# Key and query products of the recurrence in 64x64 quarters, input and result in parts of 128 rows, in a planned one-core transformer kernel

## The chip, the core and the metric

The kernel runs on one core of one Trainium2 chip. The metric is the device time of one execution in microseconds (us). Five engines work from queues of their own, in order: PE (TensorE, matrix products and transposes), DVE (VectorE), ACT (ScalarE), POOL (GpSimd) and SP (SyncE, which here only starts transfers). All data are 32-bit floats.

## The reference, cut to what matters

The input x is 8 sequences of 512 rows and 256 columns. Three blocks follow each other:

```python
x = x + 0.5 * ffn(layernorm(x))     # two layers: windowed attention, then a gated feed-forward
x = x + attn(layernorm(x))          # a linear recurrence over the 512 rows
x = x + 0.5 * ffn(layernorm(x))     # the same two layers again
```

In each of the two layers a row attends to its own and the previous window of 128 rows (8 heads of 64), and the feed-forward has 682 hidden units, which is 5 chunks of 128 and a remainder of 42. The recurrence goes, for each sequence, with keys k and queries q of length 64 and values v of length 256:

```python
def step(W, q, k, v):
    y = W @ q
    W = W - 0.01 * outer(W @ k - v, k)
    return W, y
```

The kernel does the recurrence by chunks of 128 rows: within a chunk it needs the products of all keys with all keys ("gram", 128x128) and of keys with queries ("cross", 128x128), inverts a triangular matrix made of the former, and passes W from chunk to chunk.

## The kernel before

**Who sets the order.** Every step (a product, a copy, a transfer) is a node with an engine, an assumed cost, the nodes it depends on and the buffers it takes. A list scheduler in the kernel's own Python picks at build time, one by one, the node that can start earliest by its assumed costs, shifted by a table of offsets (`EARLY`) and by a seeded perturbation that changes every 10 us of the planned time (`VARIED`). Each engine's queue is then that order, written out; on the chip nothing is reordered. Two or three of the eight sequences are in flight at once, so one sequence's attention lies beside another's feed-forward. Three `lane` tokens, three `x` buffers and two `base` buffers limit this. `load.x` brings a sequence into `x`, `again` (line 1716) brings it a second time into `base`, and `store` (line 1744) writes `base` out; all are started by SP.

**The forms of PE.** The nodes have a `kind`: "full" uses all 128 rows and 128 columns of the array, "rows" splits it into two halves of 64 rows and 128 columns, "quad" into four quarters of 64x64. The planner charges a cost for a change of kind. Before the change the kinds are:

- full: `qk` and `v` (lines 695, 782), `py` (1036), `gate` and `value` (1129), `down` (1220), the transposes of line 643, and `u`, `y`, `w` of the recurrence (1635, 1645, 1657);
- rows: the transposes `qk.turn`, `pr.turn` and `keys` (806, 948, 1403), `remains` (1231, the 42 remaining hidden units of two windows at once, one in each row half), `gram` and `cross` (1363, 1419), and `pred` (1614, W times keys in one row half and W times queries in the other);
- quad: `sc` and `po` of the attention (846, 985) and the inversion (1449, 1464).

A product of 32-bit floats is two records in the trace, a transpose is one. `gram` and `cross` are four products of 64x128 by 128 each, one for each chunk of 128 rows, all in the upper row half, with the result of all four in one PSUM bank. Keys and queries of a sequence lie in `kq`: plane 0 has keys in partitions 0 to 63 and queries in 64 to 127, plane 1 repeats the queries in partitions 0 to 63.

**Transfers of a sequence.** For the first sequence `load.x` comes in four parts of 128 rows (128 KB each), for the others as one transfer of 512 KB. `again` and `store` are 512 KB each. The scheduler assumes that a load has landed 2200 ns after its issue has ended. The lane is given back by the store. The first operations on a loaded `x` are the statistics of line 626 on DVE.

Of the kernel before, what the change touches and what calls it, by code (L numbers as in the profile page):

```python
# [11 lines left out]
AF = mybir.ActivationFunctionType  # L12
# [3 lines left out]
P = 128  # L16
# [11 lines left out]
DS = 64  # L28
# [70 lines left out]
def t_mm(n, times=1):  # L99
    return times * 2 * (n * 2 / 2.4 + 2.5)  # L100
# [14 lines left out]
def t_pool(n, spread=False):  # L115
# [103 lines left out]
VARIED = [  # L219
    37500, 31359, 15653, 39476, 20648, 53668, 22886, 22875, 25411, 5818, 50793, 17993, 43982, 49940,  # L220
    30738, 52445, 52052, 2760, 17788, 29044, 7554, 10231, 32458, 25880, 50162, 28707, 56328, 56630,
    52342, 59708, 27371, 42785, 6009, 37966, 38826, 955, 30108, 12445, 13657, 20249, 10818, 50028,
    325, 0, 7191, 46858, 11585, 55286, 8305, 0, 33660, 40052, 27704, 19753, 46446, 41995, 48233,
    15062, 296, 8963, 33350, 59233, 2924, 28516, 19956, 54218, 58660, 24722, 1205, 15080, 12783,
    47694, 13515, 37268, 33305, 11472, 21020, 39080, 49890, 42036, 14008, 22727, 3958, 1160, 24981,
    26630, 21759, 16064, 38494, 48552, 22657, 5864, 46740, 11788, 8597, 51615, 28050, 45989, 22745,
    4290, 48704, 8937, 9148, 58509, 46644, 57897, 51320, 15649, 47924, 3115, 19994, 12689, 59085,
    56246, 43769, 14414, 26360, 38246, 17633, 14501, 47748, 7399, 46997, 8397, 50340, 46088, 29559,
    15824, 19975, 28748, 1897, 45754, 59328, 27280, 16513, 19949, 41003, 25938, 12184, 59707, 33628,
    48628, 56972, 34224, 44437, 7842, 13589, 47891, 42257, 22612, 1175, 55484, 39656, 19772, 31691,  # L230
    51111, 16626, 502, 36716, 46400, 16645, 35581, 16762, 0, 45752, 57489, 16087, 51358, 28872,
    44320, 51805, 26684, 1504, 0, 45053, 54414, 48980, 14788, 27540, 29363, 53521, 4742, 57483,
    49157, 43248, 16077, 484, 34143, 50144, 14193, 1576, 18728, 4289, 59132, 46756, 27538, 40984,
    51246, 45048, 13309, 58561, 26478, 47374, 54023, 22869, 0, 30521, 59124, 44334, 56385, 9361,
    24350, 43525, 49347, 55674, 16931, 13339, 29496, 49484, 52768, 32464, 5987, 9214, 2178, 56963,
    50661, 38435, 44476, 8933, 56134, 43189, 59077, 35920, 48427, 12776, 43381, 36987, 24208, 39050,
    21677, 42532, 59957, 39253, 13094, 15624, 45940, 34800, 5277, 9793, 25563, 47184, 50569, 55023,
    28428, 22435, 50056, 23894, 1603, 18784, 56020, 42205, 52526, 56605, 11812, 42720,
]
# [188 lines left out]
def macaron_kernel(ctx: ExitStack, tc: tile.TileContext, a: dict, out: bass.AP):  # L428
# [68 lines left out]

    lane, first_x = {}, {}

    def load_x(b, w=None):  # L500

        if not w:
            lane[b], first_x[b] = Val("lane"), Val("x")
        own = slice(0, NW) if w is None else slice(w, w + 1)
        order[0] += 1
        n = node(
            "load.x",
            (-1 if b < 2 else b, order[0] if b < 2 else 0),
            "SP",
            1500.0 if w is None else 790.0,  # L510
            lambda e: dma(first_x[b].ap[:, own, :], a["x"][b].rearrange("(w p) d -> p w d", p=P)[:, own, :]),
            takes=[] if w else [lane[b], first_x[b]],
            uses=[first_x[b]] if w else [],
            tail=2200.0,
        )
        L["x", b] = [n] * NW if w is None else [*L.get(("x", b), []), n]
# [67 lines left out]
    def sequence(b):  # L584
# [469 lines left out]
        def feed_forward(x, l, ready):  # L1054
# [14 lines left out]
            for h in range(2):  # L1069
# [158 lines left out]
                def remains(pys=pys, gT=gT):  # L1228
                    for k in range(2):
                        rows = slice(k * GATE, k * GATE + REM + 1)  # L1230
                        nc.tensor.matmul(  # L1231
                            pys[k].ap[:, 0:D], gT.ap[rows, rem], w2[rows, NFC, :], start=False, stop=True
                        )

                n_d = pe("remains", t_mm(D) + 54.0, remains, [*downs, *made[NFC:]], uses=[*pys, gT], kind="rows")
                for k in range(2):
# [13 lines left out]
        def ttt(base, at):  # L1250
# [22 lines left out]
            WT = lambda: area(vb, 2 * NW * DS, 2 * NW * DS + D)  # L1273

            kq = lambda: area(vb, 2 * NW * DS + D, 2 * NW * DS + D + 2 * S).rearrange("p (i s) -> p i s", i=2)
            chunk = lambda i, w: kq()[0:DS, i, w * P : (w + 1) * P]
            on_half = lambda i, w: kq()[half(i), 0, w * P : (w + 1) * P]
            take = node("ttt.take", prio(), "SP", 0.0, lambda e: None, [*at, L["ttt"], L["rt", DEPTH - 1]], takes=[va, vb, vv])
            kqs, vs, news = [], [], []
            for w in range(NW):  # L1280
# [51 lines left out]
                def part(pk=pk, w=w):  # L1332
                    nc.scalar.activation(kq()[:, 0, w * P : (w + 1) * P], pk.ap[:, 0:P], AF.Identity, bias=bkq)
                    nc.scalar.activation(chunk(1, w), pk.ap[half(1), 0:P], AF.Identity, bias=bkq[half(1), :])

# [22 lines left out]
                )  # L1358
            pk, gram = Val("ps"), Val("ps")

            def gram_of(gram=gram):
                for w in range(NW):
                    nc.tensor.matmul(
                        gram.ap[:, w * P : (w + 1) * P], chunk(0, w), chunk(0, w), start=True, stop=True
                    )

            n_g = pe("gram", t_mm(P, 4) + 65.0, gram_of, kqs, takes=[gram], uses=[vb], kind="rows")
            gcs = [
                copy(
                    "gram.copy",  # L1370
                    H,
                    lambda r=r: g()[half(r)],
                    lambda r=r: own(as_w(gram.ap), r),
                    [n_g],
                    [],
                    [gram, va],
                )
                for r in range(2)
# [5 lines left out]
                    lambda r=r: XT()[half(1 - r), 1::2],  # L1384
                    lambda r=r: own(as_w(gram.ap), r)[:, 1::2],
                    [n_g],
                    [],
                    [gram, va],
                )
# [4 lines left out]
                t_act(H),  # L1394
                lambda: nc.scalar.mul(below(), as_w(gram.ap)[0:DS, :, half(1)], -TTT_LR),
                [n_g],
                uses=[gram, va],
            )
# [15 lines left out]
            )  # L1414
            cross = Val("ps")

            def cross_of(cross=cross):
                for w in range(NW):
                    nc.tensor.matmul(
                        cross.ap[:, w * P : (w + 1) * P], chunk(0, w), chunk(1, w), start=True, stop=True  # L1420
                    )

            bcw = lambda m: m.unsqueeze(1).to_broadcast([P, NW, m.shape[-1]])
# [54 lines left out]
            for lv in range(1, NLV - 1):  # L1478
# [116 lines left out]
            )  # L1595
            n_cr = pe("cross", t_mm(P, 4) + 65.0, cross_of, [n_1], takes=[cross], uses=[vb], kind="rows")
            n_ca = dve(
                "cross.mask",
                t_dve(S),
                lambda: nc.vector.tensor_tensor(qk(), as_w(cross.ap), bcw(upm), ALU.mult),  # L1600
                [n_cr, n_1],
                uses=[cross, va],
            )
            done, n_wt = [], None
            for w in range(NW):
# [3 lines left out]
                if w:  # L1609
                    prd, rt_ = Val("ps"), Val("row")  # L1610

                    def taken(prd=prd, pyy=pyy, w=w):
                        for i, dst in enumerate((prd, pyy)):
                            nc.tensor.matmul(  # L1614
                                dst.ap[:, 0:D], on_half(i, w), WT()[half(i)], start=True, stop=(i == 0)
                            )

                    n = pe("pred", t_mm(D) + 54.0, taken, [n_wt], takes=[prd, pyy, rt_], uses=[vb], kind="rows")
                    deps = [
# [71 lines left out]
        for half in range(2):  # L1691
# [14 lines left out]
            for l in range(DEPTH):  # L1706
                sch.stage = f"attention {half} {l}"
                ready = attention(x, l, ready)
                if half == 0 and l == DEPTH - 1:

                    again = node(
                        "again",
                        prio(),
                        "SP",
                        1500.0,
                        lambda e: dma(base.ap, a["x"][b].rearrange("(w p) d -> p w d", p=P)),
                        [ready[NW - 1]],
                        takes=[base],
                        tail=2200.0,
                    )  # L1720
# [9 lines left out]
                    [ready[w], again],  # L1730
                    uses=[base, x],
                    port=BOTH,
# [3 lines left out]
            if half == 0:  # L1736
                sch.stage = "recurrence"
                at = ttt(base, at)
        node(
            "store",  # L1740
            prio(),
            "SP",
            500.0,
            lambda e: dma(out[b].rearrange("(w p) d -> p w d", p=P), base.ap),
            at,
            uses=[base, lane[b]],
        )

    with tc.manual_schedule():
# [13 lines left out]
        for b in range(2, B):  # L1763
            load_x(b)
        for b in range(B):
# [58 lines left out]
```

## Time and profile before

| what | value |
|---|---|
| device time, three runs | 2681.55, 2684.64, 2687.15 us (median 2684.64) |
| profiled execution | 2680.98 us, span 2679.1 us |
| PE | 98% of the span, 30128 records |
| PEld (weight loads, beside PE) | 74% |
| DVE, ACT, POOL | 73%, 62%, 52% |
| PE before its first product | 7.38 us |
| result of the last sequence issued | at 2675.30 us |

The page of the profile gives each engine's busy time, the span in 40 slices, and the costliest groups of instructions: a line, an engine, output and input tiles, their count, busy time, the mean duration of one, and the idle time just before them with what ended it. Durations of PE's records overlap, because products are pipelined; what a product costs in a stream is read from one start to the next.

### The profile page before, as it was taken

What the parts mean: (1) busy time and instruction counts of PE and PEld (TensorE: products, weight loads), DVE (VectorE), ACT (ScalarE), POOL (GpSimd) and SP (SyncE); (2) the same over time, 40 slices, a digit from 0 to 9 for tenths busy, and PEclk for the clock granted to TensorE, in tenths of its full rate; (3) what the DMA queues carried; (4) which work ended last, traced back from release to release, by engine and by line L of the source; (5) the groups of instructions that cost most, each with busy time, mean ns of one, the idle gap of its engine ahead of it and who ended that gap; (6) DMA issues with size and microseconds to landing.
All of it is one profiled execution on the core that took longest, in us unless ns stands there. A gap on an engine that the chain in (4) does not pass through costs nothing. (4 is left out here: it accounts for less than half of the span.)

```text
span 2679.1 us, 76045 instructions
## 1 busy us (share of the span) xinstructions
PE 2635.0 (98%) x30128; PEld 1979.7 (74%) x30128; DVE 1953.3 (73%) x5829; ACT 1652.7 (62%) x4368; POOL 1390.4 (52%) x1985
## 2 busy tenths in 40 slices
PE   8999999999999999999999999999999999999998
PEld 5777778677777777777777777777777777777776
DVE  8777567767687768777677777687767776767765
ACT  5766565565666656666556666566645766666644
POOL 7556343635565446645447455483535645546522
PEclk9999999999999999999999999999999999999999
DMA  5000000000100010000010001000001000000000
GB/s 185 10 10 19 7 17 6 7 6 7 33 8 10 7 31 8 8 10 8 8 33 6 10 8 33 8 8 8 10 5 33 8 9 9 22 10 8 7 14 17
DMA packets 58556, 44.63 MB, mean 17 GB/s; under 512 B 7468, under 2 KB 55768, under 8 KB 58200
## 3 DMA queue, kind: packets, MB, share of 16 engines
q1 hardware_dynamic: 58200, 39.77, 4.8%
q8 instruction: 238, 3.90, 0.6%
q14 instruction: 118, 0.97, 0.1%
HBM read 18.79 MB, written 4.19 MB: 9 GB/s over the span
## 5 line engine op out<-in xcount | busy, mean ns | idle before, releaser
L1129 PE MATMUL ps<-h2T,w 128*128 128x256 f32 (+1 forms) x2816 | 649.0, 382 | 9.3 <-DVE gT L1170 3.8
L1129 PEld LDWEIGHTS ps<-h2T,w 128*128 128x128 f32 (+1 forms) x2816 | 520.0, 189 | 122.4 <-issue 21.6
L695 PE MATMUL ps<-wqkv,hT 128*128 128x512 f32 x1024 | 487.9, 600 | 0.7 <-ACT hT L607 0.2
L901 ACT ACTIVATE pr<-pr,s 128x192 f32<-128x192 f32 (+1 forms) x1024 | 440.2, 433 | 50.7 <-DVE s L889 47.6
L731 POOL TENSOR_TENSOR st<-st,powc 128x8 f32<-128x8 f32 x256 | 439.0, 1715 | 21.3
L889 DVE CUSTOM_DVE_ANT_0 pr<-ps,amask,st 128x192 f32<-128x192 f32 (+1 forms) x1024 | 356.2, 395 | 39.0 <-PE ps L846 32.0
L922 POOL TENSOR_TENSOR pr<-pr,s 128x384 f32<-128x384 f32 (+1 forms) x281 | 220.7, 794 | 214.7 <-DVE s L914 205.6
L1170 DVE SCALAR_TENSOR_TENSOR gT<-ps,b,gl 128x256 f32<-128x256 f32 x320 | 152.1, 482 | 216.5 <-PE ps L1129 179.8
L695 PEld LDWEIGHTS ps<-wqkv,hT 128*128 128x128 f32 x1024 | 183.3, 190 | 154.6 <-issue 137.5
L1220 PE MATMUL ps<-w,gT 128*128 128x256 f32 x1280 | 291.8, 380 | 0.7 <-DVE tmp L745 0.5
L714 ACT ACTIVATE tmp<-ps 128x512 f32<-128x512 f32 x256 | 152.2, 595 | 219.1 <-DVE rot L739 173.4
L1220 PEld LDWEIGHTS ps<-w,gT 128*128 128x128 f32 x1280 | 241.3, 190 | 52.5 <-issue 16.5
L1036 PE MATMUL ps<-wo,oT 128*128 128x256 f32 x1024 | 245.2, 382 | 0.0
L782 PE MATMUL ps<-wqkv,hT 128*128 128x512 f32 x512 | 240.8, 594 | 0.3 <-DVE gT L1204 0.2
L916 POOL TENSOR_TENSOR s<-s,powc 128x2 f32<-128x2 f32 x144 | 101.6, 707 | 252.6 <-ACT pr L901 246.3
L739 DVE TENSOR_TENSOR rot<-ps,rt 128x512 f32<-128x512 f32 x256 | 175.8, 687 | 74.9 <-PE ps L695 69.8
L1036 PEld LDWEIGHTS ps<-wo,oT 128*128 128x128 f32 x1024 | 192.6, 191 | 50.7 <-issue 18.3
L1151 ACT ACTIVATE gl<-ps,b 128x256 f32<-128x256 f32 x320 | 143.0, 473 | 127.6 <-PE ps L1129 125.5
L607 ACT COPY prT<-ps 128x512 f32<-128x512 f32 (+1 forms) x335 | 166.0, 556 | 59.2 <-PE ps L948 52.4
L730 POOL TENSOR_SCALAR st<-st 128x8 f32<-128x8 f32 x256 | 74.0, 289 | 247.2 <-DVE st L721 235.9
L985 PE MATMUL ps<-prT,v 64*64 64x128 f32 (+1 forms) x7168 | 193.4, 247 | 3.4 <-DVE s L889 1.5
L616 POOL TENSOR_SCALAR st<-st 128x1 f32<-128x1 f32 (+1 forms) x192 | 46.8, 244 | 285.8 <-DVE st L1077 163.4
(123 smaller groups left out, 4683.4 us busy)
## 6 DMA issues: line engine op xcount, KB each, us to landing
hs<-x SPq DMA_DIRECT2D x128, 64.0 KB
hs<-x SPq DMA_DIRECT2D x128, 63.5 KB
base<-in_x_dram SPq DMA_DIRECT2D x8, 512.0 KB
out_dram<-base SPq DMA_DIRECT2D x8, 512.0 KB
w<-in_w_dram SPq DMA_DIRECT2D x6, 640.0 KB
x<-in_x_dram SPq DMA_DIRECT2D x7, 512.0 KB
wqkv<-in_wqkv_dram SPq DMA_DIRECT2D x2, 1024.0 KB
hs<-x SPq DMA_DIRECT2D x96, 0.5 KB
```

Of the source, the lines that this page charges most:

```text
L607: (nc.scalar.copy if e == "ACT" else nc.vector.tensor_copy)(dst(), src())
L695: nc.tensor.matmul(pp.ap, hT[w].ap[:, c * P : (c + 1) * P], wqkv[:, c, i * INNER : (i + 1) * INNER], start=(c == 0), stop=(c == 1),)
L731: nc.gpsimd.tensor_tensor(ss, ss, powc[:, 0:HEADS], ALU.pow)
L739: nc.vector.tensor_tensor(heads(rot.ap), heads(pp.ap), tab, ALU.mult)
L782: nc.tensor.matmul(pv.ap, hT[w].ap[:, c * P : (c + 1) * P], wqkv[:, c, 2 * INNER : 3 * INNER], start=(c == 0), stop=(c == 1),)
L889: nc.vector.tensor_tensor_reduce(out=pr(k, nj), in0=sc.ap[:, k * 4 * DH : k * 4 * DH + nj], in1=amask[:, 0:nj] if w else amask[:, 3 * DH : ...
L901: nc.scalar.activation(pr(k, nj), pr(k, nj), AF.Exp, bias=st.ap[:, k : k + 1], scale=-1.0, accum_out=st.ap[:, 2 + k : 3 + k],)
L922: (nc.vector if e == "DVE" else nc.gpsimd).tensor_tensor(both, both, st.ap[:, 4:6].unsqueeze(2).to_broadcast([P, 2, nj]), ALU.mult)
L985: nc.tensor.matmul(po[r].ap[half(par), k * P + first : k * P + first + cols * DH], v[j].ap[half(r), hd * DH : (hd + 1) * DH], prT.ap[half( ...
L1036: nc.tensor.matmul(py.ap[:, 0:D], oT.ap[:, c, :], wo[:, c, :], start=(c == 0), stop=(c == INNER // P - 1))
L1129: nc.tensor.matmul(dst.ap[0:rows, 0 : 2 * P], w1[:, kc, col : col + rows], h2T.ap[:, kc, :], start=(kc == 0), stop=(kc == 1),)
L1220: nc.tensor.matmul(py.ap[:, 0:D], gT.ap[:, at : at + P], w2[:, c, :], start=(c == 0), stop=False)
```

## The change

`gram`, `cross`, `pred` and `remains` become "quad". `gram` and `cross` work on both row halves: the even chunks of 128 rows in the upper, the odd ones in the lower half, each cut into two halves of 64 columns, and the result goes to two neighbouring PSUM banks (even and odd chunks). For that, plane 1 of `kq` gets for odd chunks the keys in the lower half instead of the queries in the upper. `pred` and `remains` cut each of their two products into two halves of 64 columns. The copies from `gram` and `cross` read the two banks by a pattern; their number and size are unchanged. Transposes stay "rows".

The sequences from the third on are loaded in four parts of 128 rows, the second stays one transfer, and every result is written in four parts, each as soon as its 128 rows are ready. The lane is given back by the last addition to `base` instead of by the store. The assumed landing times become 2900 ns (a part), 3600 ns (a whole load) and 3300 ns (`again`). The list `VARIED` has other numbers, so the order on all engines is another one.

```diff
-            "SP", 1500.0 if w is None else 790.0,
+            "SP", 1500.0 if w is None else 450.0,
...
-            tail=2200.0,
+            tail=3600.0 if w is None else 2900.0,
...
                     for k in range(2):
                         rows = slice(k * GATE, k * GATE + REM + 1)
-                        nc.tensor.matmul(
-                            pys[k].ap[:, 0:D], gT.ap[rows, rem], w2[rows, NFC, :], start=False, stop=True
-                        )
+                        for c in range(2):
+                            cols = slice(c * DH, (c + 1) * DH)
+                            nc.tensor.matmul(
+                                pys[k].ap[cols, 0:D], gT.ap[rows, rem][:, cols], w2[rows, NFC, :], start=False, stop=True
+                            )
-                n_d = pe("remains", t_mm(D) + 54.0, remains, [*downs, *made[NFC:]], uses=[*pys, gT], kind="rows")
+                n_d = pe("remains", t_mm(D) + 54.0, remains, [*downs, *made[NFC:]], uses=[*pys, gT], kind="quad")
...
+            def by_rows(pts, other):
+                for v in range(NW // 2):
+                    for c in range(2):
+                        for e in range(2):
+                            at = slice((2 * v + e) * P, (2 * v + e + 1) * P)
+                            nc.tensor.matmul(
+                                both_of(*pts)[half(c), e, v * P : (v + 1) * P],
+                                kq()[half(e), e, at][:, half(c)],
+                                kq()[half(e), e ^ other, at],
+                                start=True, stop=True,
+                            )
...
-                    nc.scalar.activation(chunk(1, w), pk.ap[half(1), 0:P], AF.Identity, bias=bkq[half(1), :])
+                    src = half(1 - w % 2)
+                    nc.scalar.activation(
+                        kq()[half(w % 2), 1, w * P : (w + 1) * P], pk.ap[src, 0:P], AF.Identity, bias=bkq[src, :]
+                    )
...
-            n_g = pe("gram", t_mm(P, 4) + 65.0, gram_of, kqs, takes=[gram], uses=[vb], kind="rows")
+            n_g = pe("gram", t_mm(P, 2) + 65.0, lambda: by_rows(gram, 0), kqs, takes=gram, uses=[vb], kind="quad")
...
-            n_cr = pe("cross", t_mm(P, 4) + 65.0, cross_of, [n_1], takes=[cross], uses=[vb], kind="rows")
+            n_cr = pe("cross", t_mm(P, 2) + 65.0, lambda: by_rows(cross, 1), [n_1], takes=cross, uses=[vb], kind="quad")
...
                         for i, dst in enumerate((prd, pyy)):
-                            nc.tensor.matmul(
-                                dst.ap[:, 0:D], on_half(i, w), WT()[half(i)], start=True, stop=(i == 0)
-                            )
+                            for c in range(2):
+                                nc.tensor.matmul(
+                                    dst.ap[half(c), 0:D], on_half(i, w)[:, half(c)], WT()[half(i)],
+                                    start=True, stop=(i == 0),
+                                )
-                    n = pe("pred", t_mm(D) + 54.0, taken, [n_wt], takes=[prd, pyy, rt_], uses=[vb], kind="rows")
+                    n = pe("pred", t_mm(D) + 54.0, taken, [n_wt], takes=[prd, pyy, rt_], uses=[vb], kind="quad")
...
-                        tail=2200.0,
+                        tail=3300.0,
...
-                    uses=[base, x],
+                    uses=[base, x, *([lane[b]] if half and w == NW - 1 else [])],
...
-            500.0,
-            lambda e: dma(out[b].rearrange("(w p) d -> p w d", p=P), base.ap),
-            at,
-            uses=[base, lane[b]],
+        for w in range(NW):
+                450.0,
+                lambda e, w=w: dma(out[b].rearrange("(w p) d -> p w d", p=P)[:, w, :], base.ap[:, w, :]),
+                [at[w]],
+                uses=[base],
+                tail=2100.0,
...
         for b in range(2, B):
-            load_x(b)
+            for w in range(NW):
+                load_x(b, w)
```

## The prediction

> **What bounds the kernel now.** I read the busy times first, then PE's waits, then PE's stream in order of time, then the places where it stood still.
>
> ```profile
> PE 2635.0 (98%) x30128; PEld 1979.7 (74%) x30128; DVE 1953.3 (73%) x5829; ACT 1652.7 (62%) x4368; POOL 1390.4 (52%) x1985
> PEclk9999999999999999999999999999999999999999
> ```
>
> PE is the bound almost everywhere, at a full clock, and no other engine is over 73%. So a us of PE work removed is nearly a us of the time, and work that moves between the others costs nothing while they stay this far below. But 98% busy includes what PE loses in changing form. The timeline of PE in a recurrence shows it:
>
> ```profile
> 2444.54 1.88 PE L782 MATMUL ps<-wqkv,hT 128*128 128x512 f32 x4
> 2446.35 0.72 PE L948 MATMUL ps<-sq,pr 64*128 64x64 f32 x16
> 2447.00 0.46 PE L1464 MATMUL ps<-ttta,tmp 64*64 64x64 f32 x16
> 2447.39 1.98 PE L782 MATMUL ps<-wqkv,hT 128*128 128x512 f32 x4
> 2449.31 0.71 PE L806 MATMUL ps<-sq,rot 64*128 64x64 f32 x16
> ...
> 2450.23 0.85 PE L985 MATMUL ps<-prT,v 64*64 64x128 f32 x32
> 2450.90 0.63 PE L1449 MATMUL ps<-ttta,tmp 64*64 64x64 f32 x16
> ...
> 2455.24 1.11 PE L1419 MATMUL ps<-tttb 64*128 64x128 f32 x8
> 2456.28 0.68 PE L1449 MATMUL ps<-ttta,tmp 64*64 64x64 f32 x8
> ```
>
> The columns are start, length, then what. Read from start to start: the four records of `v` at 2444.54 follow another full product and take 1.81 us; the same four at 2447.39, entered from quarters and left for halves, take 1.92. Within a run of full products four take 1.72, so leaving costs about 0.09 and entering about 0.10. `po` does 16 products of 64x64 with 128 columns or fewer (32 records) in 0.67 us, four quarters at once. `cross` needs 1.04 us for eight records in one row half, where nothing runs beside it.
>
> ```profile
> PE ps L643 <- DVE x L634: 10.9, 5, 7.4
> PE ps L1129 <- DVE gT L1170: 3.8, 3, 1.8
> PE ps L948 <- POOL pr L922: 3.0, 4, 1.1
> PE ps L1129 <- DVE s L889: 2.9, 1, 2.9
> ```
>
> PE's own waits (sum, times, longest) are few: 7.4 us at the start and some large ones later. The large ones have one origin. DVE and PE at the third sequence's entry, and the windows around it (PE busy, PEld, DVE, ACT, POOL, then clock):
>
> ```profile
> 722.32 0.43 DVE L626 BATCH_NORM_STATS2 st<-x 128x6 f32<-128x256 f32 x1 [3.62 <-DMA x<-in_x_dram]
> ```
>
> ```profile
> 725.25 4.54 PE L1129 MATMUL ps<-h2T,w 128*128 128x256 f32 x12 [2.86 <-DVE s L889]
> ```
>
> ```profile
> 722.00:726.00 4.00, 1.14 (x5) 0.64 (x4) 3.54 (x16) 3.23 (x7) 2.61 (x8) 0.96 0.07 21
> 726.00:730.00 4.00, 4.00 (x14) 3.25 (x13) 2.69 (x8) 1.94 (x5) 0.68 (x2) 0.61 0.05 12
> ```
>
> The 512 KB load was issued at 716.89 and DVE, in order, stood on it until 722.32; PE ran dry for 2.86 us, and then had a clock of 0.61 for a while. Loads of this kind took 5.3 to 5.8 us from issue at four such places.
>
> **The change part by part.** The working is against the profiled execution, 2680.98 us (span 2679.1, the rest outside it); the median of three is 3.66 higher.
>
> *Price list.* I laid the trace's PE records beside PE's queue as built: both have the same 621 stretches of one form. I fitted each stretch's length, start to start, by its counts and one term for the form it is entered from, least absolute deviation. One 64x128 product in quarters costs 0.0551 us (four at once), one product of `gram` or `cross` 0.236, one of `remains` or `pred` 0.243 (two at once, 0.485 a pair). Entering costs: quad to full 0.182, full to rows 0.149, rows to quad 0.153, full to quad 0.151, rows to full 0.193, quad to rows 0.148. The sum is 2608.0 us for 2666.4 measured from first to last record: 55 us net is left as stalls.
>
> *Gram and cross.* 64 products at 0.236 = 15.1 us go; 128 quarter products at 0.0551 = 7.1 come. **-8.0**. By starts alone, 16 x 4 records x 0.112 = 7.2. They are in PE's stream, so this is on the path. The second PSUM bank that they hold can delay other products; that is in the last term below.
>
> *Remains and pred.* 88 pairs at 0.485 = 42.7 go. Each becomes four quarters of 256 columns; twice `po`'s price is 0.110 each, 0.441 for four, 38.8 in all: **-3.9**. No 256-column quarters run in this trace. Bounds: 0 if their weights show as bare as now (0.272 against 0.213 us between the two records of a half), -5.2 if none of that 0.059 stays.
>
> *Changes of form.* I counted them in PE's queue as built, before to after: quad to full 169 to 163, full to rows 156 to 130, rows to quad 107 to 117, full to quad 88 to 69, rows to full 74 to 35, quad to rows 26 to 22; 620 to 536. Priced: -1.1 - 3.9 + 1.5 - 2.9 - 7.5 - 0.6 = **-14.4**. This is the largest term. It holds as far as a price from 620 cases holds.
>
> *Loads in parts.* Four load stalls of PE (2.86, 1.69, 1.77, 2.72 us) and the half clock behind two of them (3.4 us each, half of it lost) make 12.4 us. In DVE's queue after the change, the work between the last addition to `base` and the first statistics of the new x is 3.5, 3.7, 1.3, 2.9 and 4.1 us, by row durations; before 5.5, 3.1, 3.4, 4.9 and 2.6. So DVE does not come later. But a part moves 128 KB instead of 512, and the last store's packets took 1.66 us for 512 KB, so the first part is there about 1.2 us sooner. Two of the stalls should shrink to nothing and the others by half: **-6**; bounds -12.4 and +3 (SP now issues up to four stores and four loads, 0.46 us each, where it issued two transfers, and the row shifts of another sequence queue behind them; DVE waited 10.8 us for those before).
>
> In the Trainium skill, "DMA: Bandwidth & Descriptors", section "Measured", transfers should be batched to 1 MiB or more, and its "Anatomy of one DMA" puts a fixed 2.0 us on each: paid one after another on five loads, three more parts would give +30 and a time of about 2688, an estimate from that page. The trace shows four parts issued in 1.86 us at the start, one behind the other, so I leave it out of the sum.
>
> *Start.* Two sequences now begin in parts ahead of the weights, and DVE does eight pairs of statistics before the first scaling instead of four. At 0.53 us a pair from 4.72 us the first transpose comes near 9.4 instead of 7.38; the first rotation follows two projections earlier in the queue, which gives most of it back. **+1** (0 to +2).
>
> *End.* The last store is issued at 2675.30 and ends the span 3.8 us later. A quarter of the 1.66 us of packets is left behind the last addition: **-1.2** (0 at worst).
>
> *Small waits.* Some 40 of the 55 us left over are spread over hundreds of stretches. The new order has its own. I take **0**, bounds a quarter of it, -10 and +10. ACT hands 36 copies to DVE, DVE 48 products to POOL; at 73% and 52% this is covered, and both kernels load ACT's table 178 times.
>
> Sum: -8.0 - 3.9 - 14.4 - 6 + 1 - 1.2 = -32.5 us: 2648.5 against the profiled execution, 2652 against the median.
>
> **The rivals.** *Quarters that do not overlap (slower).* If two quarters of one row half run one after the other, `remains` and `pred` need a second 0.426 us each, 88 x 0.426 = +37.5 instead of -3.9, and `gram` and `cross` save nothing. With the other terms: +37.5 - 14.4 - 6 + 1 - 1.2 = +17, about 2702. The change turns slower when two thirds of the overlap are lost. Against it speaks `po`: its third and fourth quarter share a row half with the first and second, and 32 records still fit in 0.67 us. For it: there the row halves alternate, while `remains` and `pred` give both quarters of the upper half first.
>
> The Trainium skill, "TensorE: Matmul & The Clock Gate", "Part 3: Packing small matmuls", says that a weight load overlaps running products only when the row group differs. By that rule 2702 would be the answer; the 0.67 us of `po` contradict it for quarters of 64x64.
>
> *A new order that starves PE (no change).* If the planner, with its other numbers and two more banks in the recurrence, leaves 20 to 26 us of new stalls, most of the 26 us of removed PE work returns as idle time: 2672 to 2685. For it: every queue is another one, and one 512 KB load of five stays. Against: the four big stalls came from landing times taken too short, and these are now longer.
>
> *Loads in parts bring nothing.* The PE terms stay: 2658, inside the range.
>
> **How the numbers follow.** Forecast with its bounds 0.80, starving 0.12, quarters in series or anything else that costs as much 0.08. The range goes from 2638 (all of the load stalls and some small waits gone) to 2671 (loads no better, small waits 10 us worse, `remains` unchanged). A difference under 0.2%, 5.4 us, is not told from none. Half of the starving case is still faster by more: faster 0.87, same 0.05, slower 0.08.
>
> **What would show it.** Right: `gram` and `cross` in 16 records of which four start together, near 0.5 us a call; `remains` and `pred` four starts within 30 ns and 0.43 us to the next; 536 changes of form; PE busy near 2605 us; DVE waits on `x` under 7 us; the last store's landing under 3 us. Wrong: a second quarter that starts only when the first ends; PE's idle time above 60 us; new large waits on `ps` banks or POOL.

## The result, and the profile after

| kernel | median | runs | ratio to before |
|---|---|---|---|
| before | 2683.65 us | 2681.55 to 2687.15 (4 runs) | 1 |
| after | 2651.18 us | 2650.45 to 2654.59 (4 runs) | 0.988, 95% interval 0.9863 to 0.9897 |
| after, a second series | 2651.63 us | 2650.78 to 2654.51 | 0.9881, 0.9866 to 0.9896 |

The change makes the kernel 32.5 us faster by the medians. The profiled execution of after took 2654.59 us (span 2652.8), the slowest of its series, so that profile against profile only 26.3 us of span are gone; the second series' profile has a span of 2649.5. Medians of one kernel lie up to 2 us apart between series, so differences of 3 us between experiments stand at the edge of what can be told.

The second series has this expectation:

> The changed kernel unaltered, to compare others with on one chip. Both theories: 2650 to 2655 us, within 0.2% of its earlier median 2651.2.

The busy times and the clock on the page of after:

```profile
PE 2612.1 (98%) x30608; PEld 1963.9 (74%) x30608; DVE 1944.2 (73%) x5811; ACT 1638.2 (62%) x4332; POOL 1435.2 (54%) x2039
PEclk9999999999999999999999999999999999999999
```

PE is busy 22.9 us less and is still the bound. The stretch from its first to its last record shrank from 2666.4 to 2639.6 us (-26.8); ahead of it lie 8.83 us instead of 7.38 (+1.46), behind it 4.35 instead of 5.29 (-0.9). These three make the 26.3.

The new quarters, in PE's timeline (start, length, line, shapes, records), first a `remains` and then a `gram` of after:

```profile
1093.69 1.57 PE L988 MATMUL ps<-prT,v 64*64 64x128 f32 x64
1095.08 0.61 PE L1236 MATMUL ps<-w,gT 43*64 43x256 f32 x8
1095.52 1.52 PE L849 MATMUL ps<-kT,qT 64*64 64x128 f32 x64
```

```profile
2390.38 1.10 PE L849 MATMUL ps<-kT,qT 64*64 64x128 f32 x32
2391.30 0.62 PE L1292 MATMUL ps<-tttb 64*64 64x128 f32 x16
2391.84 5.47 PE L1132 MATMUL ps<-h2T,w 128*128 128x256 f32 x24
```

From its start to the next one `remains` takes 0.44 us for four quarters of 256 columns, and no change of form lies on either side. The single records of this call start at 0, 6, 13 and 19 ns, the second four at 220 to 239 ns, the next product at 435 ns. `gram` takes 0.54 us, the leaving of its form included, where before eight records took 1.04; its records start in fours, from 0, 109, 218 and 327 ns on. This call is a clean one. From start to next start the eight calls of `gram` take 0.55 to 0.69 us; those of `cross` take 0.49 to 1.23 us, because records of the inversion or short waits stand inside them.

PE's own waits and DVE's waits on transfers (sum, times, longest):

```profile
PE ps L646 <- DVE x L637: 9.0, 2, 8.8
PE ps L849 <- ACT qT L610: 3.5, 14, 0.7
...
PE ps L1132 <- ACT gl L1154: 2.1, 2, 1.0
```

```profile
DVE st L629 <- DMA x<-in_x_dram: 6.0, 6, 2.9
```

The same wait of DVE in before:

```profile
DVE st L626 <- DMA x<-in_x_dram: 15.0, 6, 4.7
```

Behind the 8.8 us of the start no wait of PE is longer than 1.7 us. The four stalls of 1.7 to 2.9 us at the entries of sequences are gone, and of the three stretches of half clock inside the run (3.41 us each) one is left, and none in the second series. DVE's wait on `x` fell from 15.0 us to 6.0 (7.6 in the second series).

The start, where after loses, in the timelines of PE and DVE (the last bracket: idle before, and what ended it):

```profile
8.83 1.97 PE L646 MATMUL ps<-sq,x 128*128 128x128 f32 x8 [8.83 <-DVE x L637]
12.47 2.04 PE L698 MATMUL ps<-wqkv,hT 128*128 128x512 f32 x2 [1.67 <-DMA wqkv<-in_wqkv_dram]
```

```profile
15.10 2.36 DVE L544 TENSOR_TENSOR rt<-gT,ttta 128x1024 f32<-128x1024 f32 x2 [3.00 <-DMA gT<-in_rope_dram]
```

Before, the same two rows were:

```profile
10.15 6.40 PE L695 MATMUL ps<-wqkv,hT 128*128 128x512 f32 x12
10.44 2.36 DVE L541 TENSOR_TENSOR rt<-gT,ttta 128x1024 f32<-128x1024 f32 x2 [0.82 <-DMA gT<-in_rope_dram]
```

Four more parts of `x` stand ahead of the weights and of the rotation's table on SP's queue. And the end of after:

```profile
2647.77 0.66 PE L1236 MATMUL ps<-w,gT 43*64 43x256 f32 x8
2649.58 0.81 SPq L1771 DMA_DIRECT2D out_dram<-base  x2
```

### The profile page after: what moved, and what is told of

Read it like the earlier page. It is cut to its first block, busy times and chain, and to the rows that moved or that the text cites. A ratio compares the mean times of both kernels' runs of the same rounds, so it can differ in the third digit from the quotient of the medians.

```text
span 2652.8 us, 77020 instructions
## 1 busy us (share of the span) xinstructions
PE 2612.1 (98%) x30608; PEld 1963.9 (74%) x30608; DVE 1944.2 (73%) x5811; ACT 1638.2 (62%) x4332; POOL 1435.2 (54%) x2039
## 4 chain that ended last, share of the span: by engine, by line
PE 93%; DVE 3%; ACT 2%; issue 1%; POOL 1%; DMA 0%; SPq 0%; DVEq 0%; ACTq 0%; POOLq 0%
PE ps L1132 23%; PE ps L698 16%; PE ps L1223 10%; PE ps L1039 8%; PE ps L785 8%; PE ps L988 6%; PE ps L849 6%; PE ps L951 4%; PE ps L809 3%; PE ps L646 3%; PE ps L1236 1%; PE ps L1368 1%; PE ps L1479 1%; PE ps L1464 1%; PE ps L1660 1%
## 5 line engine op out<-in xcount | busy, mean ns | idle before, releaser
L925 POOL TENSOR_TENSOR pr<-pr,s 128x384 f32<-128x384 f32 (+1 forms) x324 | 255.6, 799 | 272.8 <-DVE s L917 239.1
L610 ACT COPY prT<-ps 128x512 f32<-128x512 f32 (+1 forms) x320 | 159.0, 551 | 109.7 <-PE ps L951 108.2
L849 PE MATMUL ps<-kT,qT 64*64 64x128 f32 (+1 forms) x7168 | 194.2, 250 | 6.4 <-ACT qT L610 3.5
```

The costliest lines, as they stand in the source:

```text
L849: nc.tensor.matmul(sc[par].ap[half(c), k * 4 * DH + at : k * 4 * DH + at + keys.stop - keys.start], qT.ap[half(par), 2 * g + k, half(c)], ...
L925: (nc.vector if e == "DVE" else nc.gpsimd).tensor_tensor(both, both, st.ap[:, 4:6].unsqueeze(2).to_broadcast([P, 2, nj]), ALU.mult)
```

## The experiments

All times are medians, all ratios are against the kernel before on the same chip, and "over after" means over the 2651.6 us of the second series. The kernels with halves, one row half, whole loads and transfers from ACT's queue ran on another chip than the second series; before took 2683.9 us on the one and 2683.2 on the other.

**Remains and pred in halves.** The two steps are emitted as before the change, in the order of after; that gives 584 changes of form instead of 536.

```diff
-                        for c in range(2):
-                            nc.tensor.matmul(dst.ap[half(c), 0:D], on_half(i, w)[:, half(c)], WT()[half(i)], ...)
+                        nc.tensor.matmul(dst.ap[:, 0:D], on_half(i, w), WT()[half(i)], ...)
...
```

> The changed kernel, with remains and pred given out as halves of 64x128 again, in the same order on every engine. Theory (a quarter product costs no less by itself; what it saves is a change of form beside sc, po and the inversion): PE's queue then has 584 changes of form instead of 536, by the fitted prices 94.7 us against 87.4, +7.3, and 88 pairs at 0.485 instead of 0.443 us, +3.7: +11 us, about 2662. Rival (the new order alone makes the gain, the form of these 88 pairs is worth nothing): within 3 us of the changed kernel, 2648 to 2654.

2656.05 us, ratio 0.9899 (0.9885 to 0.9914): 4.4 over after, between the two. The busy times of after's second series and of this kernel:

```profile
PE 2609.7 (98%) x30608; PEld 1962.3 (74%) x30608; DVE 1945.5 (73%) x5811; ACT 1633.1 (62%) x4332; POOL 1434.9 (54%) x2039
PE 2616.6 (99%) x30256; PEld 1964.2 (74%) x30256; DVE 1944.3 (73%) x5811; ACT 1633.0 (62%) x4332; POOL 1435.7 (54%) x2039
```

PE is busy 6.9 us longer and idle 3.3 us less (spans 2649.5 and 2653.1), so part of the additional work fills time in which PE would have waited. Fitted as in the prediction and set against after's first profile, the terms for changes of form are 96.4 us instead of 86.5, the products of the two steps 43.0 instead of 39.0, and what the fit leaves as stalls 41.4 instead of 44.7. That makes +10.6, but PE's stretch from first to last record is no longer than in that profile (2639.3 against 2639.6): the fit must have given some 11 us less to the other products. So it moves about as much between the changes of form and the products beside them as the changes are said to cost, and the price of the 48 changes does not show in the time: the 4.4 us are hardly more than what the two steps' own products cost (4.0).

**Gram and cross in one row half.** All quarters of these two steps go to the upper row half, and plane 1 of `kq` has the queries there for every chunk.

```diff
-                                kq()[half(e), e, at][:, half(c)],
-                                kq()[half(e), e ^ other, at],
+                                kq()[half(0), 0, at][:, half(c)],
+                                kq()[half(0), other, at],
...
-                    src = half(1 - w % 2)
+                    src = half(1)
...
```

> The changed kernel, with all quarters of gram and cross in the upper row half, in the same order: two column quarters share one row half. Theory (column quarters of one row half run at the same time): 8 rounds of 0.112 us a call instead of 4, +0.45 us on 16 calls, +7 us, about 2658, and four starts come in pairs. Rival (a row half takes one product after another): 16 rounds, +1.34 us a call, +21 us, about 2672.

2657.02 us, 0.9902 (0.9887 to 0.9917): 5.4 over after. The same call as above, in this kernel's timeline:

```profile
2394.36 1.10 PE L849 MATMUL ps<-kT,qT 64*64 64x128 f32 x32
2395.29 1.09 PE L1292 MATMUL ps<-tttb 64*64 64x128 f32 x16
2396.31 3.95 PE L1132 MATMUL ps<-h2T,w 128*128 128x256 f32 x17
```

1.02 us instead of 0.54: two quarters at a time, in one row half and different column halves. They do overlap, since sixteen records of 0.11 us each one after the other would be 1.8 us; but they do not start in pairs, as expected: from the third on the records of this call start singly, 52 to 57 ns apart. All sixteen calls of `gram` and `cross` together, from start to next start, take 16.6 us in before, 11.8 in after and 17.7 here, and these 5.9 us are about the 5.4 of the time. So the two row halves bring these steps their gain, and the rival in which quarters of one row half run in series falls.

**Whole loads.** The loads from the third sequence on are 512 KB again (one of them stays in parts), in the order of after: where the first part was issued the whole sequence is, and the other three parts are not issued.

```diff
-            lambda e: dma(first_x[b].ap[:, own, :], a["x"][b].rearrange("(w p) d -> p w d", p=P)[:, own, :]),
+            lambda e: (
+                dma(first_x[b].ap, a["x"][b].rearrange("(w p) d -> p w d", p=P))
+                if b in taken and w == 0 and b != 4
+                else None
+                if b in taken and b != 4
...
```

> The changed kernel, with the sequences from the third on loaded in one transfer of 512 KB again (the sequence that starts first stays in parts), issued where the first part was, in the same order. Theory (the first part lands sooner and DVE stands less): DVE's wait on x grows from 6 us to 10 us or more, PE loses 3 to 6 us with the half clock behind it, 2654 to 2657. Rival (assumed landing times in the planner did it, the parts nothing): within 2 us of the changed kernel.

2652.1 us, 0.9883 (0.9866 to 0.9899): 0.5 over after, no difference. In DVE's waits of this kernel:

```profile
DVE st L635 <- DMA x<-in_x_dram: 10.1, 9, 2.9
```

DVE stands on `x` for 10.1 us instead of 6.0 (7.6 in the second series), and the time does not show it. The parts of the later loads are not what removed the stalls.

**The order alone.** The three edits above at once: the products in their old forms, whole loads, in the order of after, with its longer assumed landing times and its results in parts.

> The changed kernel in its own order, with three things undone at once: remains and pred as halves, gram and cross with all quarters in the upper row half, and loads of 512 KB from the third sequence on. What is left against the kernel before is the new order with its longer assumed landing times, and stores in parts. Theory (forms and order add up; the forms are worth about 10 us here, the parts of the loads nothing): 4.4 + 5.4 + 0.5 us above the changed kernel, 2660 to 2664, so the order alone is worth about 21 of the 32 us. Rival (the losses hide each other in the same waits): 2654 to 2658.

2664.78 us, 0.9932 (0.992 to 0.9945), and before beside it 2682.41. So the order, with the results in parts, is worth about 18 us, and the three edits 13.1 (4.4, 5.4 and 0.5 singly, 10.3). The page of this kernel shows what the order does:

```profile
PE 2625.0 (99%) x30256; PEld 1970.2 (74%) x30256; DVE 1943.9 (73%) x5811; ACT 1633.4 (61%) x4332; POOL 1435.8 (54%) x2039
```

Against the profile of before, PE is idle 6.7 us less (37.4 instead of 44.1, in a span of 2662.4) and busy 10.0 less. Of the latter an estimated 5.1 is half of the three stretches of half clock, of which none is left inside this run; the other 5 lie near the price of the changes of form, of which this order with the old forms has 584 instead of 620 (94.7 us instead of 101.8). So most of the order's gain is stalls and what followed them.

**The list of random numbers.** `VARIED` only perturbs the planner's choices, so I gave the kernel before 300 plain random numbers, and then the same numbers together with the new forms of products alone. The planner orders all queues anew in both.

```diff
-    37500, 31359, 15653, 39476, ...
+    (300 other random numbers)
```

> The kernel before, with its list VARIED replaced by random numbers, so that the planner orders every queue anew. PE's queue then has 1062 changes of form instead of 620; nothing else is added. Theory (a change of form costs its fitted price in any order): priced 174.8 us against 101.8, +73 us, and some more small waits: 2745 to 2785. Rival (the price fits only where few changes stand, or they hide in waits): +30 us or less, under 2715.

> The kernel before with the same random list as the run beside it, and of the change only the forms: gram, cross, remains and pred in quarters; loads and stores are as before. PE's queue has 1056 changes of form, 6 fewer. Theory (the forms save the work of gram and cross and little else; the fall from 620 to 536 belongs to the new list): 8 us for gram and cross, 4 for the pairs, 2 for the changes of form, 8 to 16 us faster than its neighbour, plus or minus the waits of another order. Rival (the forms themselves remove the changes of form, as the change's largest term supposes): 25 us faster or more.

3078.52 us, 1.1471 (1.1454 to 1.1488), and with the new forms 3065.77, 1.142 (1.1383 to 1.1457). The first missed every expectation: 395 us over before, where the 442 additional changes of form were priced at 73. The page and PE's waits of the first show where it is:

```profile
PE 2837.8 (92%) x30128; PEld 2049.4 (67%) x30128; DVE 1950.4 (63%) x5816; ACT 1661.4 (54%) x4372; POOL 1386.0 (45%) x1990
PEclk9998999999999999999999999999999999998998
```

```profile
PE ps L928 <- POOL pr L902: 22.3, 21, 6.9
PE ps L623 <- DVE x L614: 21.9, 7, 9.5
PE ps L965 <- ACT prT L587: 18.4, 25, 1.5
```

PE is idle for 242 us instead of 44. Its busy time grew by 203: some 73 by the priced changes of form, and an estimated 87 by the clock, because 36 stretches of half clock, 234 us in all, follow the waits (the mean granted clock is 0.962 instead of 0.998). PE works through 184 us of them, and half of that is lost, less the 5 of before. The other 40 or so stay open. The second came out in its range: 12.8 us less with the forms alone, at 1056 changes instead of 1062. Its page:

```profile
PE 2825.7 (92%) x30608; PEld 2024.6 (66%) x30608; DVE 1944.7 (63%) x5789; ACT 1697.4 (55%) x4421; POOL 1392.9 (45%) x1982
```

That the forms are worth these 12.8 us is not shown by this pair: the intervals touch, the executions of the second kernel lie between 3058 and 3077 us, its order is another one, and it has 32 stretches of half clock, 208 us, instead of 36 with 234. What the pair does show is that the forms by themselves do not bring fewer changes of form. How many changes there are belongs to the pair of forms and list: with the lists exchanged the two kernels as built have 1023 and 945, with their own 620 and 536.

**Three other starts.** Since the start had grown, I tried to get the old one back: the first transfers of weights and the rope table issued by ACT's queue; the first 82 steps in another order; and the first sequence alone ahead of the weights, the second behind them. The last two are put in another order after the planner has given out the buffers, so nothing ensures that values are read before they are written over. The second computes other values, and its time only shows where the waits fall.

```diff
+    FIRST = (("qk", 0), "rope", ("v", 0))
...
+        if name in FIRST:
+            for dst, src in pairs:
+                nc.scalar.dma_start(dst, src)
```

> The changed kernel, with the first four weight transfers (wqkv of layer 0 in two pieces, scales, rope) issued from ACT's queue at once instead of from SP's behind eight parts of x. Theory (at the start PE and DVE wait for an issue that stands late in SP's queue, 4.97 and 5.95 us): the first qk product starts at about 11 us instead of 12.5, the rope table is there before DVE asks for it at 12.1 instead of 15.1, and the time falls by 2 to 4 us, 2647 to 2649. Rival (the transfers share the same 16 engines, so the parts of x come later and the first transpose with them): no gain, or up to 1 us worse.

> The changed kernel, with only its start written in another order: the four parts of the first sequence's x and the identity stay first, then wqkv, scales and rope, then the second sequence's parts; DVE scales the first sequence before it takes the statistics of the second, and PE turns the second sequence's rows after the first qk.turn. From about 30 us on, every queue is as in the changed kernel. Theory (the new start costs 4 us against the one before, through wqkv issued at 4.97 us and eight statistics before the first scaling): the first qk product starts at 8.5 to 10 us instead of 12.5, the first qk.turn 3 us earlier, and what PE gains there stays to the end because PE bounds: 3 to 5 us faster than the changed kernel. Rival (the gain is given back at the next wait, for the values' weights or for the second sequence): within 1 us of the changed kernel.

> The changed kernel, with a milder change of its start: first sequence's parts, identity, wqkv, scales, rope, then the second sequence's parts on SP; on DVE the first sequence is scaled before the second's statistics; PE's order keeps all four first transposes ahead of qk. Theory (the weights stood too late in SP's queue): first qk product at about 11.2 us instead of 12.5, rope used at 12.5 instead of 15.1, 1 to 2.5 us faster than the changed kernel. Rival (the second sequence's parts now come behind 1.8 MB, and all four transposes wait for them): first qk at 12 us or later, no gain.

2654.76 us (0.9893, 0.9878 to 0.9908), 2659.0 (0.9905, 0.989 to 0.992) and 2654.75 (0.9898, 0.9883 to 0.9913): 3.1, 7.4 and 3.1 over after. None of the three gains anything. In the first, DVE gets the second part of `x` at 6.97 us instead of 3.48, behind 1 MB of weights (between 2.8 and 5.2 us only their packets move), and PE's first product goes to 14.46:

```profile
6.97 0.43 DVE L635 BATCH_NORM_STATS2 st<-x 128x6 f32<-128x256 f32 x1 [3.21 <-DMA x<-in_x_dram]
```

```profile
14.46 1.97 PE L652 MATMUL ps<-sq,x 128*128 128x128 f32 x8 [14.46 <-DVE x L643]
```

In the second the projections start early, at 8.81, and then PE runs dry at the second sequence:

```profile
8.81 5.84 PE L707 MATMUL ps<-wqkv,hT 128*128 128x512 f32 x8 [0.79 <-DMA wqkv<-in_wqkv_dram]
...
24.18 1.12 PE L655 MATMUL ps<-sq,x 128*128 128x128 f32 x4 [3.50 <-DVE x L646]
```

In the third that sequence's first part is there only at 12.81 us, and the first projection, queued behind both sequences' transposes, starts at 16.37, 3.9 later than in after; 3.1 of it shows at the end.

## Why the prediction was right, point by point

The total was right (2652 against 2651.18) and the likeliest case came true, but that it came so close is luck: several terms were off in both directions and balanced. Measured with the same fit:

| term | predicted | measured | why |
|---|---|---|---|
| gram and cross | -8.0 | -5.2 | 0.0776 us a quarter product in the fit instead of 0.0551 |
| remains and pred | -3.9 | -3.7 | 0.1108 instead of 0.110 |
| changes of form | -14.4 | -15.3 | 101.8 to 86.5 us |
| prices of other products | none | +11 | transposes +4.7, inversion +3.2, attention +3.3 |
| loads, stalls and small waits | -6 | -16 | left over -13.7, in which 2.3 lost at the start are counted with the start |
| start | +1 | +3.8 | 1.46 ahead of the first product, 2.3 after it |
| end | -1.2 | -0.9 | |

The sum is -26.3, that of the two profiles. The prediction's -32.5 stood against a profile 2.7 us under its median and was shifted to the median; that shift hit because after's profile lies 3.4 over its own. The fit leaves 2666.4 - 2608.0 = 58.4 us of before, from which the -13.7 is taken, and not the 55 that the prediction names. Of its signs one missed: PE is busy for 2612.1 us (2609.7 in the second series), not near 2605.

**Gram and cross** were mis-sized. The clean calls of `gram` run at the predicted price (0.54 us less the 0.09 of leaving is 0.45, or 0.056 a quarter). But most calls of `cross` are interleaved with a step of the inversion: from start to next start the calls of `gram` together take 3.4 us less than before, those of `cross` 1.3, which makes -4.7. The fit shares that out over all calls. By the experiment with one row half, half of the overlap is worth 5.4 us.

**Remains and pred** were right, and so was the choice of value between the bounds: nothing of the weight loads shows.

**Changes of form**: the number was right, and the fit's term fell by nearly what was forecast. But the largest term of the sum is not confirmed by that, because the fit does not hold the price of a change apart from the price of the products beside it. In this table -15.3 and +11 stand together and make -4, where -14.4 was forecast. In the halves experiment the fit gave 9.9 back to the changes and took some 11 from the other products, and the time grew by 4.4, with 4.0 for the two steps' own products. So the step "it holds as far as a price from 620 cases holds" says too little: the price is not the time at the end. With 442 more changes it was far too small, because that order also waits.

**Other products** were assumed to keep their prices. Eleven us of them came back; a fit can put there what it takes from the changes of form, or short waits between neighbours, so which of these it is stays open.

**Loads in parts**: the stalls went, to the far end of the bound (9.0 us of idle time and two half clocks, some 12), but not for the reason given. The experiment with whole loads loses nothing, and DVE's wait of 10.1 us stays hidden. The stalls left with the new order, its longer assumed landing times and the results in parts; which of these counts was not separated.

**Start** was mis-sized, and by a queue: the sum followed DVE's statistics to the first transpose, and I did not follow the four additional parts past the weights and the rope table on SP's queue. The trace shows them 2.3 and 4.7 us later.

**The rivals.** *Quarters that do not overlap* fell: starts 6 to 7 ns apart. With it falls for these products the rule of the Trainium skill's "TensorE: Matmul & The Clock Gate", "Part 3", that a weight load overlaps only a product of another row group: in the kernel with one row half all quarters of a call are of one row group, and its weight loads start while its products run (a product at 2395.452 us with a record of 269 ns, a load at 2395.453). *An order that starves PE* did not happen (idle 40.7 us instead of 44.1), but the random list shows what an order can cost: 395 us, far more than the 20 to 26 that were put on it. (Those 20 to 26 on top of 2652 are 2672 to 2678; the prediction's 2685 does not follow from them.) *Loads in parts bring nothing* is true of the parts and false of the time, since the order gave what the parts were credited with.

For batching, the estimate of 2688 worked out in the prediction from "DMA: Bandwidth & Descriptors" did not show: whole loads and loads in parts lie 0.5 us apart. That page took its figures from transfers that GpSimd issued; here SP issues them all.

## What to carry to other kernels

A kernel with a planned order has to be compared with its order held still: here the order is worth 18 us and the edits 13, and in the diff the order is little more than a list of numbers and a few assumed times. A term that a fit gives has to be tested by an experiment that changes it alone: the changes of form were the largest term of the sum, and taking 48 of them back cost no more than the products that came with them. Any transfer that is put ahead at the start moves every transfer behind it on that queue, and each of those has to be followed to its first reader.

## What the runs showed of the hardware that I had not expected

- Four quarters of 64x64 start 6 to 7 ns apart, two of them in the same row half, with 256 columns as with 128; two quarters in one row half overlap as well (sixteen records in 1.02 us, the single starts 52 to 57 ns apart).
- A wait can cost more than its length. In the kernel with random numbers 36 stretches of half clock cover 234 us of 3080, and in the 4 us ahead of each of the 35 that lie within PE's work PE had stood still for 1.2 to 3.0 us, in one piece or several. Before has three such stretches inside the run, behind 1.6 to 2.9 us of idle time; two of its waits, of 1.7 and 1.8 us, had none behind them.
- A transfer of 1 MB issued from another engine's queue delays small ones on SP's: the second part of `x`, 128 KB, reached DVE 3.5 us later, and for 2.4 us only packets of the large one moved.
